# Two graph-attention and feed-forward layers on one core: the rates of the feed-forward's first normalisation move to ScalarE and GpSimd, and its draining slots leave the written order

## The chip, the cores and the metric

The kernel runs on one core of a Trainium2 chip, as one launch. The metric is the device time of that launch in microseconds (us). A core has five engines with their own instruction queues: TensorE (PE in the profile; its weight loads are PEld), VectorE (DVE), ScalarE (ACT), GpSimd (POOL) and SyncE (SP), which here only issues transfers. Each queue is worked off in order, and engines wait for each other through semaphores.

## The reference

The input `x` has 4096 rows of 256 numbers, the adjacency matrix `adj` is 4096 x 4096. There are two layers, each a graph attention and a feed-forward, both with a residual and with a layer normalisation ahead:

```python
x = x + L0_gnn(layernorm(x), adj)      # 4 heads of 64, masked softmax
x = x + L0_ffn(layernorm(x))           # the stage that is changed
x = x + L1_gnn(layernorm(x), adj)      # two attentions, one after the other
x = x + L1_ffn(layernorm(x))           # router, 2 of 6 experts per row
```

The feed-forward of layer 0 is a recurrence of 30 steps on each row, with one weight matrix `W` (256 x 256):

```python
def step(h):
    h = h + 0.01 * tanh(h)
    h = h * sigmoid(h)                                   # Silu
    h = (h - mean) * rsqrt(var + 1e-5) * ln_w + ln_b     # over the 256 columns
    return h @ W.T + b
```

Rows don't influence one another in this stage. Its input is `layernorm(x1)`, where `x1` is the output of the first attention.

## The kernel before

**Tiling.** A tile is 128 rows (one per partition) by 256 columns. Four tiles make a group (`G = 4`, 512 rows), eight groups make the whole input (`NG = 8`). In the feed-forward a *unit* is one step of one group: `units = 30 * 8 = 240`, unit `u` works on group `u % 8`. The state of all rows stays in the buffer `y`, scaled by 100.

**Slots.** The loop over `at` (246 slots) is a software pipeline. In slot `at` unit `at` begins (Tanh on ScalarE at L861, the addition `th` on GpSimd at L862); unit `at - 2` goes through Silu (L850), a scaled float16 copy of its right half (L852), the remainder of that copy on VectorE (L853, called `lower`), a transposing transfer on SP's queue (L857), and its statistics (L874 and L876, VectorE); unit `at - 3` has its left half transposed on TensorE (L831) and copied out of PSUM (L881, ScalarE), and its rate (variance plus eps) to the power of -0.5 formed (L884 ScalarE, L885 and L886 GpSimd); unit `at - 4` is multiplied by the weights (L896 in float32, L899 in float16); unit `at - 5` is written to `y` (L838, VectorE). Slots 0 to 7 are the first pass over the groups, in which the later stages fill; slots 240 to 245 drain.

**First normalisation.** Before its first Tanh a group must be normalised into `y`. `load(g)` takes the rows of `x1` from DRAM (SP's queue, four buffers in the pool `stream`, shared with other stages); `measure(g)` calls `over_std`: statistics (L101, L103), the addition of eps (L105) on VectorE, the power (L106) on GpSimd; `init(g)` makes `rs` (times 100, L726) and `nm` (minus mean times `rs`, L728) on VectorE, then four activations write `y` (L730, ScalarE). Groups 0 and 1 are measured ahead of the loop; in slot `at`, `init(at + 1)` stands ahead of `measure(at + 2)`.

**Weight preparation.** Ahead of the loop VectorE and TensorE fold `ln_w` and `ln_b` into the weights and find a power of two to scale them (L749 to L805). The first scaled copy (L852 of unit 0) needs that `scale`. Parts of the preparation, the end of the first attention and the first slots share VectorE's queue.

**Order.** Around the slot loop stands `tc.manual_schedule` for PE, DVE, ACT and POOL: these engines' queues get the instructions in the order in which the loop writes them. Outside it a planner decides, from its own costs and due times, the order in each queue. SP isn't in the list. `add_manual_dep` makes the addition at L862 wait for `lower` of the unit two before, with the reason "the port that both use".

**The drain.** For the units of the last step, `y` is written with the residual's scale, `load(u % NG)` brings `x1` back, GpSimd adds it (L912) and SP stores the sum to `x2d` (L913), from which the next attention loads its rows (L93).

Of the kernel before, what the change touches and what calls it, by code (L numbers as in the profile page):

```python
# [11 lines left out]
F32 = mybir.dt.float32  # L12
BF16 = mybir.dt.bfloat16
F16 = mybir.dt.float16
I32 = mybir.dt.int32
AF = mybir.ActivationFunctionType
OP = mybir.AluOpType
# [4 lines left out]
P = 128  # L22
C = 256
# [4 lines left out]
G = 4  # L28
EPS = 1e-5
# [15 lines left out]
def gnn_ffn_kernel(ctx: ExitStack, tc: tile.TileContext, a: dict, out: bass.AP):  # L45
    nc = tc.nc
# [3 lines left out]
    NG = NT // G  # L50
    GR = G * P
# [30 lines left out]
    def rows_of(t, g):  # L82
        return t[g * GR : (g + 1) * GR, :].rearrange("(r p) c -> p r c", p=P)
# [12 lines left out]
    def over_std(pool, src):  # L96

        st = pool.tile([P, G, 6], F32, name="ln_st")
        mv = pool.tile([P, G, 2], F32, name="ln_mv")
        for r in range(G):  # L100
            nc.vector.bn_stats(st[:, r, :], src[:, r, :])  # L101
        for r in range(G):
            nc.vector.bn_aggr(mv[:, r, :], st[:, r, :])  # L103
        rstd = pool.tile([P, G], F32, name="ln_rstd")
        nc.vector.tensor_scalar(rstd, mv[:, :, 1], EPS, None, op0=OP.add)  # L105
        nc.gpsimd.tensor_tensor(rstd, rstd, mhalf, OP.pow)  # L106
        return rstd, mv
# [588 lines left out]
    with ExitStack() as scope:  # L696
# [2 lines left out]
        w16 = one.tile([P, 2, C], F16, name="w16")  # L699
        scale = one.tile([P, 2], F32, name="scale")  # L700
        under = one.tile([P, 2, G], F32, name="under")
        eps = one.tile([P, 1], F32, name="eps")
        nc.gpsimd.memset(eps, EPS)
        bias = one.tile([P, C], F32, name="bias")
        last = one.tile([P, C], F32, name="last")
        y = one.tile([P, NT, C], F32, name="y")
# [5 lines left out]
        def load(g):  # L712
            if g not in ahead:
                load_ahead(x1d, g)
            x1[g] = ahead.pop(g)

        measured = {}

        def measure(g):
            measured[g] = over_std(small, x1[g])  # L720

        def init(g):
            t = x1.pop(g)
            rstd, mv = measured.pop(g)
            rs = small.tile([P, G], F32, name="rs")
            nc.vector.tensor_scalar(rs, rstd, 100.0, None, op0=OP.mult)  # L726
            nm = small.tile([P, G], F32, name="nm")
            nc.vector.scalar_tensor_tensor(nm, mv[:, :, 0], -1.0, rs, op0=OP.mult, op1=OP.mult)  # L728
            for r in range(G):
                nc.scalar.activation(  # L730
                    y[:, g * G + r, :], t[:, r, :], AF.Identity, scale=rs[:, r : r + 1], bias=nm[:, r : r + 1]
                )

        for g in range(3):
            load(g)
        with tc.tile_pool(name="f_prep", bufs=1) as prep, tc.tile_pool(name="f_pps", bufs=1, space=PSUM) as pps:
            ln = prep.tile([2 * KC, P], F32, name="ln")
# [2 lines left out]
            wr = prep.tile([P, KC, C], F32, name="wr")  # L740
            nc.scalar.dma_start(wr, a["L0_ffn_W"].rearrange("(k p) c -> p k c", p=P))
            nc.scalar.dma_start(bias, bcast_rows(a["L0_ffn_b"]))
            measure(0)
            init(0)
            measure(1)
            ps = pps.tile([P, 2 * KC], F32, name="ps_ln")
            nc.tensor.transpose(ps, ln, ident[: 2 * KC, : 2 * KC])
            lnT = prep.tile([P, 2 * KC], F32, name="lnT")
# [63 lines left out]

        th, zs, mvs, rs, zT, zT16, pos = {}, {}, {}, {}, {}, {}, {}
        units = FFN_STEPS * NG
        with tc.manual_schedule(
            engines={
                mybir.EngineType.PE,
                mybir.EngineType.DVE,
                mybir.EngineType.Activation,
                mybir.EngineType.Pool,  # L820
            }
        ):
            for at in range(units + 6):
                if at + 3 < NG:
                    load(at + 3)
                u = at - 3
                if 0 <= u < units:
                    z = zs.pop(u)
                    pt = ps_t.tile([P, GR], F32, name="tp")
                    for r in range(G):  # L830
                        nc.tensor.transpose(pt[:, r * P : (r + 1) * P], z[:, r, :P], ident)  # L831
                u = at - 5
                if 0 <= u < units:
                    g = u % NG
                    po, rstd = pos.pop(u), rs.pop(u)
                    end = u >= units - NG
                    for r in range(G):
                        nc.vector.scalar_tensor_tensor(  # L838
                            y[:, g * G + r, :],
                            po[:, r, :],  # L840
                            rstd[:, r : r + 1],
                            last if end else bias,
                            op0=OP.mult,
                            op1=OP.add,
                        )
                u = at - 2
                lower = None
                if 0 <= u < units:
                    z = zs[u] = work.tile([P, G, C], F32, name="z")
                    nc.scalar.activation(z, th.pop(u), AF.Silu, scale=0.01)  # L850
                    z16 = work.tile([P, 2, G, P], F16, name="z16", bufs=4)
                    nc.scalar.activation(z16[:, 0], z[:, :, P:], AF.Identity, scale=scale[:, :1])  # L852
                    lower = nc.vector.scalar_tensor_tensor(  # L853
                        z16[:, 1], z[:, :, P:], scale[:, :1], z16[:, 0], op0=OP.mult, op1=OP.subtract
                    )
                    zT16[u] = work.tile([P, 2 * G, P], F16, name="zT16", bufs=4)
                    nc.sync.dma_start_transpose(zT16[u], z16.rearrange("p s r c -> p (s r c)"))  # L857
                if at < units:
                    g = at % NG
                    th[at] = work.tile([P, G, C], F32, name="th", bufs=4)  # L860
                    nc.scalar.activation(th[at], y[:, g * G : (g + 1) * G, :], AF.Tanh, scale=0.01)  # L861
                    ins = nc.gpsimd.tensor_tensor(th[at], th[at], y[:, g * G : (g + 1) * G, :], OP.add)  # L862
                    if lower is not None:
                        tc.add_manual_dep(
                            ins.ins,
                            lower.ins.name,
                            mybir.DependencyInfo(mybir.DependencyClass.Sync, mybir.DependencyReason.DATA),
                            reason="the port that both use",
                        )
                if 0 <= u < units:  # L870
                    st = small.tile([P, G, 6], F32, name="z_st")
                    mv = small.tile([P, G, 2], F32, name="z_mv")
                    for r in range(G):
                        nc.vector.bn_stats(st[:, r, :], z[:, r, :])  # L874
                    for r in range(G):
                        nc.vector.bn_aggr(mv[:, r, :], st[:, r, :])  # L876
                    mvs[u] = mv
                u = at - 3
                if 0 <= u < units:
                    zT[u] = work.tile([P, GR], F32, name="zT")  # L880
                    nc.scalar.copy(zT[u], pt)  # L881

                    rs[u] = small.tile([P, G], F32, name="z_rs")
                    nc.scalar.activation(rs[u], mvs.pop(u)[:, :, 1], AF.Identity, bias=eps)  # L884
                    nc.gpsimd.tensor_tensor(rs[u], rs[u], mhalf, OP.pow)  # L885
                    nc.gpsimd.tensor_tensor(rs[u], rs[u], under[:, int(u >= units - NG), :], OP.mult)  # L886
                if at + 1 < NG:
                    init(at + 1)
                if at + 2 < NG:
                    measure(at + 2)  # L890
                u = at - 4
                if 0 <= u < units:
                    src, src16 = zT.pop(u), zT16.pop(u)
                    po = pos[u] = ps_o.tile([P, G, C], F32, name="po")
                    for r in range(G):
                        nc.tensor.matmul(po[:, r, :], src[:, r * P : (r + 1) * P], wT, start=True, stop=False)  # L896
                        for part in range(2):
                            for other in range(2):
                                nc.tensor.matmul(  # L899
                                    po[:, r, :],  # L900
                                    src16[:, part * G + r, :],
                                    w16[:, other, :],
                                    start=False,
                                    stop=(part == 1 and other == 1),
                                )
                    if u >= units - NG:
                        load(u % NG)
                u = at - 5
                if units - NG <= u < units:
                    g = u % NG  # L910
                    t = x1.pop(g)
                    nc.gpsimd.tensor_tensor(t, t, y[:, g * G : (g + 1) * G, :], OP.add)  # L912
                    nc.sync.dma_start(rows_of(x2d, g), t)  # L913


    RH = a["L1_ffn_router_w1"].shape[1]
# [456 lines left out]
```

## Time and profile before

| | us |
|---|---|
| median of 3 runs | 3432.09 (3427.78 to 3432.75) |
| profiled execution, own time | 3432.09 |
| its span, on which all profile times lie | 3430.3 |
| feed-forward: first init to last addition of rows | 800.0 to 1797.5 |
| filling: first init to the steady pace | 800 to about 865 |
| steady pace, per unit | 3.92 |
| draining: last Tanh to the first transpose of the next attention | 1765.03 to 1795.90 |

In the profile's rows a line reads: start (us from the span's start), duration, engine, line of the kernel, operation, output<-inputs, shapes, count; in brackets the idle time of the engine just before and what ended it. In the chain of waits the columns are start, length and what was running. Durations of neighbours on one engine overlap by some 0.1 us, so a sum over a queue is made from starts.

### The profile page before, as it was taken

The numbers are of one execution on the slowest core, as the hardware profiler recorded it, in microseconds if no ns is written. First come the engines' busy times: TensorE is split into PE (matmuls) and PEld (weight loads), VectorE is DVE, ScalarE is ACT, GpSimd is POOL, SyncE is SP. The second block draws the span as 40 slices with busy tenths as digits, with TensorE's granted clock in tenths as the row PEclk, the third lists the DMA queues.
The fourth block names the chain that finished last, engine by engine and source line by source line (L and its number), as shares of the span: only waits on it lengthen the run. The fifth ranks groups of instructions, "written<-read, shape, count | busy, mean of one in ns | idle before, by whom it ended". The sixth has DMA issues, their size and how long they took to land.

```text
span 3430.3 us, 84143 instructions
## 1 busy us (share of the span) xinstructions
PE 3156.7 (92%) x34367; PEld 2771.3 (81%) x34367; DVE 3115.3 (91%) x6016; ACT 2754.3 (80%) x3414; POOL 1242.3 (36%) x1149
## 2 busy tenths in 40 slices
PE   7889999996999999999988999999989999985995
PEld 4788888884888888888876999999779999983884
DVE  7999999998999999999988999999889999996445
ACT  3888888896888888888866999999799999982221
POOL 3211100003999999999992000000200000002662
PEclk9999999997999999999999999999999999996997
DMA  7997886603333333333354031230503041314224
GB/s 146 173 228 152 184 184 142 192 22 77 68 67 68 69 69 69 69 69 68 67 140 147 22 123 58 90 118 24 167 24 124 27 136 43 120 46 145 88 91 185
DMA packets 533658, 351.62 MB, mean 103 GB/s; under 512 B 350589, under 2 KB 483866, under 8 KB 533274
## 3 DMA queue, kind: packets, MB, share of 16 engines
q1 hardware_dynamic: 452210, 287.12, 30.4%
q0 software_dynamic: 73920, 52.97, 9.9%
q10 hardware_dynamic: 7144, 6.16, 0.6%
q8 instruction: 271, 4.44, 0.5%
q14 instruction: 113, 0.93, 0.1%
HBM read 248.01 MB, written 68.81 MB: 92 GB/s over the span
## 4 chain that ended last, share of the span: by engine, by line
PE 36%; DVE 35%; issue 13%; POOL 7%; ACT 6%; DMA 2%; DVEq 0%; POOLq 0%; ACTq 0%; SPq 0%
DVE m L617 17%; PE acc L569 10%; PE po L899 9%; PE po L896 9%; ACT st L483 4%; DVE rows L632 3%; PE tp L831 2%; DVE m L632 2%; POOL th L862 2%; PE ph L1262 1%; POOL yd L1293 1%; DVE z_st L874 1%; DVE y L838 1%; POOL gx L1227 1%; DVE u L496 1%
## 5 line engine op out<-in xcount | busy, mean ns | idle before, releaser
L569 PE MATMUL acc<-vals,m 128*128 128x130 f16 (+1 forms) x19456 | 1722.4, 233 | 72.0 <-DVE m L632 42.5
L483 ACT ACTIVATE st<-f1b,f2b 128x1024 bf16<-128x1024 f32 (+2 forms) x1664 | 1659.1, 1073 | 98.8 <-DVE m L617 92.1
L569 PEld LDWEIGHTS <-m 128*128 128x128 bf16 x19456 | 1517.3, 98 | 170.2 <-DVE m L632 64.8
L617 DVE TENSOR_TENSOR m<-st,m 128x2048 bf16<-128x2048 bf16 (+2 forms) x832 | 929.1, 1134 | 15.2 <-ACT st L483 14.9
L569 PE MATMUL acc<-vals,rows 128*128 128x130 f16 x5120 | 614.1, 221 | 15.1 <-DVE rows L632 15.1
L899 PE MATMUL po<-w,zT 128*128 128x256 f16 x3840 | 580.4, 274 | 5.7 <-DMA zT<-z 5.7
L896 PE MATMUL po<-wT,zT 128*128 128x256 f32 x1920 | 579.1, 384 | 6.4 <-ACT zT L881 6.4
L862 POOL TENSOR_TENSOR th<-th,y 128x1024 f32<-128x1024 f32 x240 | 568.8, 2370 | 38.4 <-ACT th L861 14.8
L899 PEld LDWEIGHTS <-zT 128*128 128x128 f16 x3840 | 377.6, 98 | 169.7 <-DMA zT<-z 7.3
L569 PEld LDWEIGHTS <-rows 128*128 128x128 bf16 x5120 | 490.0, 96 | 20.5 <-DVE rows L632 20.1
L632 DVE TENSOR_TENSOR rows<-m,m 128x2048 bf16<-128x2048 bf16 x320 | 391.7, 1224 | 10.2
L838 DVE SCALAR_TENSOR_TENSOR y<-po,z_rs,bias 128x256 f32<-128x256 f32 x928 | 384.8, 477 | 4.2 <-PE po L899 2.1
L874 DVE BATCH_NORM_STATS2 z_st<-z 128x6 f32<-128x256 f32 x960 | 335.5, 412 | 0.0
L896 PEld LDWEIGHTS po<-wT,zT 128*128 128x128 f32 x1920 | 292.5, 193 | 16.4 <-ACT zT L881 7.8
L106 POOL TENSOR_TENSOR ln_rstd<-ln_rstd,mhalf 128x4 f32<-128x4 f32 x32 | 42.1, 1317 | 656.8 <-DVE ln_rstd L105 641.9
L850 ACT ACTIVATE z<-th 128x1024 f32<-128x1024 f32 x240 | 251.2, 1046 | 7.3 <-POOL th L862 6.6
L209 POOL DMA_DIRECT2D rows<-in_adj_dram x80 | 72.9, 912 | 492.9 <-PE tp_m L219 479.4
L861 ACT ACTIVATE th<-y 128x1024 f32<-128x1024 f32 x240 | 249.8, 1041 | 0.1
L885 POOL TENSOR_TENSOR z_rs<-z_rs,mhalf 128x4 f32<-128x4 f32 x240 | 244.5, 1019 | 0.0
L881 ACT COPY zT<-tp 128x512 f32<-128x512 f32 x240 | 140.8, 587 | 116.2 <-PE tp L831 116.2
L632 DVE TENSOR_TENSOR m<-m,m 128x1792 bf16<-128x1792 bf16 (+1 forms) x200 | 202.2, 1011 | 13.0 <-PE acc L569 0.5
L462 POOL MEMSET hs<- 128x4 f32 x3 | 0.3, 103 | 582.4 <-DVE u L513 582.3
(246 smaller groups left out, 3159.1 us busy)
## 6 DMA issues: line engine op xcount, KB each, us to landing
m<-edges SPq DMA_DIRECT2D x32, 2048.0 KB
rows<-in_adj_dram POOLq DMA_DIRECT2D x64, 448.0 KB
edges<-ms SPq DMA_DIRECT2D x64, 448.0 KB
m<-edges SPq DMA_DIRECT2D x16, 1792.0 KB
f1b<-fd SPq DMA_DIRECT2D x32, 512.0 KB
rows<-x1d SPq DMA_DIRECT2D x16, 512.0 KB
y<-yd SPq DMA_DIRECT2D x16, 512.0 KB
f1b<-fd SPq DMA_DIRECT2D x16, 448.0 KB
```

Of the source, the lines that this page charges most:

```text
L483: nc.scalar.activation(steps[at][:, s, :w], f1b[c, h][:, :w], AF.Relu, bias=f2b[:, 2 * q + s, h : h + 1], scale=BIG)
L569: nc.tensor.matmul(acc[:, i, cols], lhs[:, s, rows], v[:, cols], start=(j == 0 and n_ == 0), stop=(j == NT - 1 and n_ == 1), skip_group_ch ...
L617: nc.vector.tensor_tensor(m1[:, :, :w], st[:, :, :w], m, OP.logical_and if turned(q) else OP.min)
L632: nc.vector.tensor_tensor(m2[:, :, :w], m, m1[:, :, :w], OP.subtract)
L838: nc.vector.scalar_tensor_tensor(y[:, g * G + r, :], po[:, r, :], rstd[:, r : r + 1], last if end else bias, op0=OP.mult, op1=OP.add,)
L850: nc.scalar.activation(z, th.pop(u), AF.Silu, scale=0.01)
L861: nc.scalar.activation(th[at], y[:, g * G : (g + 1) * G, :], AF.Tanh, scale=0.01)
L862: ins = nc.gpsimd.tensor_tensor(th[at], th[at], y[:, g * G : (g + 1) * G, :], OP.add)
L874: nc.vector.bn_stats(st[:, r, :], z[:, r, :])
L885: nc.gpsimd.tensor_tensor(rs[u], rs[u], mhalf, OP.pow)
L896: nc.tensor.matmul(po[:, r, :], src[:, r * P : (r + 1) * P], wT, start=True, stop=False)
L899: nc.tensor.matmul(po[:, r, :], src16[:, part * G + r, :], w16[:, other, :], start=False, stop=(part == 1 and other == 1),)
```

## The change

The statistics of a group stay on VectorE (`measure`), but what follows them is a new function `rate`: one activation on ScalarE scales the variance and eps by 1e-4 (so that the power gives 100 times the rate), and three GpSimd operations form the power, mean times rate, and its negative. VectorE's three small operations per group are gone. `measure`, `rate` and `init` of one group now stand in three successive slots, so the statistics are taken one slot earlier and groups 0 to 2 ahead of the loop; `load(3)` goes ahead too. The loop's body becomes a function `slot(at)`, the same but for these calls; slots 0 to 239 are called inside `tc.manual_schedule`, slots 240 to 245 after it, so that the planner orders them.

```diff
-        eps = one.tile([P, 1], F32, name="eps")
-        nc.gpsimd.memset(eps, EPS)
+        eps = one.tile([P, 2], F32, name="eps")
+        nc.gpsimd.memset(eps[:, :1], EPS)
+        nc.gpsimd.memset(eps[:, 1:], EPS * 1e-4)
...
-        measured = {}
+        measured, rates = {}, {}
 
         def measure(g):
-            measured[g] = over_std(small, x1[g])
+            st = small.tile([P, G, 6], F32, name="x_st")
+            mv = measured[g] = small.tile([P, G, 2], F32, name="x_mv")
+            for r in range(G):
+                nc.vector.bn_stats(st[:, r, :], x1[g][:, r, :])
+            for r in range(G):
+                nc.vector.bn_aggr(mv[:, r, :], st[:, r, :])
+
+        def rate(g):
+
+            mv = measured.pop(g)
+            rs = small.tile([P, G], F32, name="x_rs")
+            nc.scalar.activation(rs, mv[:, :, 1], AF.Identity, scale=1e-4, bias=eps[:, 1:])
+            nc.gpsimd.tensor_tensor(rs, rs, mhalf, OP.pow)
+            nm = small.tile([P, G], F32, name="x_nm")
+            nc.gpsimd.tensor_tensor(nm, mv[:, :, 0], rs, OP.mult)
+            nc.gpsimd.tensor_scalar(nm, nm, -1.0, None, op0=OP.mult)
+            rates[g] = rs, nm
 
         def init(g):
             t = x1.pop(g)
-            rstd, mv = measured.pop(g)
-            rs = small.tile([P, G], F32, name="rs")
-            nc.vector.tensor_scalar(rs, rstd, 100.0, None, op0=OP.mult)
-            nm = small.tile([P, G], F32, name="nm")
-            nc.vector.scalar_tensor_tensor(nm, mv[:, :, 0], -1.0, rs, op0=OP.mult, op1=OP.mult)
+            rs, nm = rates.pop(g)
...
-        for g in range(3):
+        for g in range(4):
             load(g)
...
-            measure(0)
+            for g in range(3):
+                measure(g)
+                if g < 2:
+                    rate(g)
             init(0)
-            measure(1)
...
+        def slot(at):
+            if 0 < at and at + 3 < NG:
+                load(at + 3)
...
+                nc.scalar.activation(rs[u], mvs.pop(u)[:, :, 1], AF.Identity, bias=eps[:, :1])
...
+            if at + 2 < NG:
+                rate(at + 2)
+            if at + 1 < NG:
+                init(at + 1)
+            if at + 3 < NG:
+                measure(at + 3)
...
-            for at in range(units + 6):
-                if at + 3 < NG:
-                    load(at + 3)
...
-                if at + 1 < NG:
-                    init(at + 1)
-                if at + 2 < NG:
-                    measure(at + 2)
...
+            for at in range(units):
+                slot(at)
+
+        for at in range(units, units + 6):
+            slot(at)
```

In the queues as built, TensorE's order is the same as before throughout, and GpSimd's is the same from the end of the filling on. In the drain ScalarE's Silu of units 238 and 239 stands ahead of the copies of 236 and 237, VectorE's `lower` of 238 and 239 ahead of the writing of `y` for 235 and 236, and on SP the transposing transfer of unit 239 ahead of the load of rows for group 6. `load(3)` is at the same place in SP's queue as before.

## The prediction

> **What bounds the kernel now.** I read the stage windows first, to see where the feed-forward leaves its own pace. Columns: stretch, length, busy time of each engine with its instructions, granted TensorE clock, DMA share, GB/s.
>
> ```profile
> core 0: us, PE busy (x) PEld busy (x) DVE busy (x) ACT busy (x) POOL busy (x), PEclk, DMA share, GB/s
> 800.00:840.00 40.00, 19.00 (x72) 12.12 (x72) 32.98 (x119) 25.32 (x41) 20.10 (x16) 0.59 0.37 93
> 840.00:880.00 40.00, 33.14 (x196) 25.03 (x197) 34.55 (x114) 33.16 (x51) 28.18 (x24) 0.87 0.38 86
> 1000.00:1200.00 200.00, 200.00 (x1430) 163.80 (x1429) 199.35 (x664) 173.82 (x256) 191.21 (x154) 1.00 0.39 68
> ...
> 1750.00:1800.00 50.00, 40.57 (x262) 31.59 (x261) 37.64 (x120) 21.46 (x34) 45.40 (x34) 0.92 0.67 186
> ```
>
> From 880 to 1750 TensorE never rests: 3.92 us per unit (866 us of the stage), untouched by the change. What can move are the filling slots (800 to 865) and the draining ones (1765 to 1796).
>
> In ScalarE's timeline one filling slot runs from Silu to Silu, 832.31 to 839.73, 7.41 us:
>
> ```profile
> 832.31 1.04 ACT L850 ACTIVATE z<-th 128x1024 f32<-128x1024 f32 x1
> 833.38 0.72 ACT L852 ACTIVATE z<-z,scale 128x512 f16<-128x512 f32 x1
> 834.01 1.04 ACT L861 ACTIVATE th<-y 128x1024 f32<-128x1024 f32 x1
> 834.96 0.56 ACT L881 COPY zT<-tp 128x512 f32<-128x512 f32 x1
> 835.42 0.30 ACT L884 ACTIVATE z_rs<-z_mv,eps 128x4 f32<-128x4 f32 x1
> 837.74 2.08 ACT L730 ACTIVATE y<-rows,nm,rs 128x256 f32<-128x256 f32 x4 [2.02 <-DVE nm L728]
> ```
>
> 2.02 us are a wait for `nm`. VectorE's timeline shows why, with GpSimd's addition below it:
>
> ```profile
> 803.31 2.31 DVE L726 TENSOR_SCALAR rs<-ln_rstd 128x4 f32<-128x4 f32 x1 [0.33 <-POOL ln_rstd L106]
> ...
> 809.21 2.24 DVE L728 SCALAR_TENSOR_TENSOR nm<-ln_mv,rs 128x4 f32<-128x4 f32 x1
> ...
> 836.40 1.11 DVE L726 TENSOR_SCALAR rs<-ln_rstd 128x4 f32<-128x4 f32 x1
> ```
> ```profile
> 803.24 2.35 POOL L862 TENSOR_TENSOR th<-th,y 128x1024 f32<-128x1024 f32 x1
> ...
> 835.13 2.35 POOL L862 TENSOR_TENSOR th<-th,y 128x1024 f32<-128x1024 f32 x1 [1.95 <-ACT th L861]
> 837.44 1.01 POOL L885 TENSOR_TENSOR z_rs<-z_rs,mhalf 128x4 f32<-128x4 f32 x1
> 838.53 0.20 POOL L886 TENSOR_TENSOR z_rs<-z_rs,under 128x4 f32<-128x4 f32 x1
> ```
>
> A 0.17 us operation lasts until GpSimd's 2.35 us addition ends. So each slot closes a ring: init (ACT), Silu, scaled copy, `lower` and statistics (DVE), `rs` held to the end of `th` (POOL), `nm`, next init. The early stalls (2.31, 2.24) also lie in VectorE's queue ahead of the weight preparation, whose `scale` is done at 818.46; the first scaled copy waits 2.63 us for it (starts 818.56).
>
> The chain of waits for the drain:
>
> ```profile
> 1784.88 2.31 POOL rows L912
> 1787.21 4.11 DMA x2d<-rows
> 1791.33 4.43 DMA rows<-x2d
> 1795.90 1.96 PE tp L114 x8
> ```
>
> Before 1784.88 it runs through GpSimd alone, gapless from 1756.90 in its timeline.
>
> **The filling, part by part.** Removed from VectorE per group: L105, L726, L728 (0.17, 0.17, 0.15 unblocked). Added: on ScalarE one 128x4 activation (nearest row L884: 0.30, of which 0.20 until the next starts); on GpSimd a multiplication (nearest L886: 0.20, next about 0.1 later) and a tensor_scalar (no row in the filling; the 128x16 tensor_scalar of the attention, L337, is 0.27 free and 1.31 blocked). The power stays. I take 0.25 and 0.3 with their gaps; both at a power's price (1.02, next 1.1 later) would add 1.65 to a slot's GpSimd sum.
>
> (a) *Preparation.* In VectorE's new order the first statistics end at 801.2 (before 801.9: 0.49 us of waiting and four small operations are gone), but a third group comes in ahead of the weights and a fourth right after `lbb` (4 x 0.33 + 0.28 = 1.6 each), so `lbb` is done at 803.8 against 802.97. `th` of unit 0 moves from 803.24 to about 804.1, behind two groups' rates on GpSimd. The first L765 (TENSOR_SCALAR, 128x256) arrives at 805.2 and, like L726, is held to 806.45; the second runs at 807.5, the mean's matmuls end at 809.1 (1.23 after it, as before), L772 at 810.8 (held by `th` of unit 1), its matmuls 2.08 later, then the same chain: `scale` at 816.2, gain 2.3. If L763 or L770 falls under the second `th`, 1.5 us of it are lost; I set off 0.8. The loads of groups 4 to 6 wait for init to free a buffer; before, the first is issued at 802.17 and its data have moved by 806, so its statistics at 806.9 don't wait. Group 3's load is only written earlier: on SP it already stood ahead.
>
> (b) *Slots.* init of group g takes its rates from the slot before, so the 2.70 us idle ahead of init at 822.92 and the 2.02 of the later slots go. The slot becomes ScalarE's own sum of starts: 1.07 + 0.63 + 0.95 + 0.47 + 0.20 + 0.20 (new) + 2.0 = 5.52. Slot 3 (Silu at 824.91 before) starts at 816.2 + 0.7 + 0.95 + 0.2 + 2.0 = 820.1. Four slots, 4 x 5.52, reach slot 7 at 842.2 (before 854.55): 12.4 us. Is another engine slower? GpSimd: 2.35 + 1.1 + 0.25 + 1.1 + 0.25 + 0.3 = 5.35. VectorE: 1.6 (y) + 0.67 + 1.6 + 1.6 = 5.5 at most. Rates are done 2.7 + 2.35 + 3.0 = 8.05 after their slot's start and wanted at 5.52 + 3.5 = 9.0: 1 us of slack, which hides the three GpSimd operations; without it each us is a us per slot.
>
> (c) *TensorE's clock.* Before, the last filling unit ran slow:
>
> ```profile
> 855.64 0.65 PE L831 MATMUL tp<-ident,z 128*128 128x128 f32 x4 [1.50 <-ACT z L850]
> 857.81 1.22 PE L896 MATMUL po<-wT,zT 128*128 128x256 f32 x2 [1.52 <-ACT zT L881]
> 858.83 1.06 PE L899 MATMUL po<-w,zT 128*128 128x256 f16 x4
> ```
>
> Pairs of groups take 1.7 instead of 0.87, so unit 4 (857.81) cost 6.95 and unit 5 began at 864.76. After: unit 4 begins when zT is copied, 842.2 + 1.07 + 0.63 + 0.95 + 0.57 = 845.4; at full clock unit 5 follows at 849.4, 15.4 us earlier than 864.76, and the steady pace carries that to the end. At the slow clock from unit 3 on, unit 5 comes near 854.3: gain 10.4. The row: slow periods began after 3.7 us with only 0.65 us of work in them (two gaps of 1.5); after one gap of 1.52 at 848.88 it stayed fast. The Trainium skill ("TensorE: Matmul & The Clock Gate", HAM oscillation) asks only that no idle gap exceed some 3.4 us; by that these slow periods should not be there, and neither would any after. By the row, what counts is the share of work in such a stretch: 3.9 of 5.5 us from now on, so fast too, but with less certainty. By the page 15.4, by the row's pessimistic reading 10.4; I take fast.
>
> A second rule speaks against moving work to GpSimd: "SBUF — State Buffer" (two separate sides) says that the port pair of VectorE and GpSimd is an exclusive lock for a whole instruction. The rows agree: in steady state L886 takes 0.41 instead of 0.20 beside `lower` (0.74). By the free rows the three operations cost the slot nothing; by the rule up to 0.7 us once a slot, inside the 1 us of slack, so again nothing.
>
> **The drain.** TensorE's and GpSimd's orders there are unchanged. ScalarE puts Silu of 238 ahead of 236's zT copy: copy from 1766.56 to 1770.4, and L896 from 1770.28 to 1771.0, hidden since L899 waits for zT's transfer to 1771.43. 237's copy comes after Silu of 239 (1771.04 to 1777.3): L899 starts 1778.3 instead of 1777.80, hidden by the next transfer at 1784.64; uncovered it is 0.5. VectorE puts `lower` ahead of `y` twice, but GpSimd's additions hold `lower` to about the old times, and the `y` behind it (up to 3 us late) is wanted by GpSimd only at 1784.83. On SP the last transposing transfer passes a 512 KB load (0.46): perhaps 1 us for unit 239, yet what follows it (rows added at 1795.15, stored 1797.53) is the last group of the next stage; the load then is 2 us late for an addition at 1790.7. The chain through 1787.21 doesn't feel any of it. I take 0, between -1.5 and +1.
>
> **Sum.** 15.4 - 0.8 + 0 = 14.6 us. Profiled: span 3430.3, own time 3432.09 (1.8 around it), equal to the median of three. 3432.1 - 14.6 = **3417.5 us**.
>
> **Rivals.** *A, slow clock from unit 3* (0.17): gain 10.4 - 0.8 = 9.6, 3422.5. For: it fell back twice in this stretch; against: 74% work. *B, GpSimd becomes the bound* (0.08): nm, neg at a power's price and locked by `lower`, slot 5.35 + 1.65 + 0.7 = 7.7, as long as before; what stays is (a), the init wait of slot 2 and unit 4: 2.3 + 2.5 + 3.0 - 4 x 0.3 - 0.8 = 5.8, 3426.3. *C, slower* (0.03): the same queue, each of the new operations held as L726 was, by 2.3 us. Gain turns to loss at 4 x (X - 7.41) > 7.0, a slot of X = 9.2, and is a measurable loss from 10.9; three holds of 2.3 give 5.35 + 6.9 = 12.3 and 3432 - 7 + 19.6 = 3444.7. Against: VectorE has no locking operation over 0.75 us in a slot. *D, the drain gives too* (0.07): the transfer's 1.5 us reach the chain, 3416. The forecast itself: 0.65, own range 3413 to 3420.
>
> **Numbers.** 0.2% (6.9 us) is about what a measurement here tells from no change. Forecast, A and D are faster: 0.89; B same: 0.08; C slower: 0.03. The range of eight in ten reaches up to A with 1.5 us more (3424), and down by the 4.3 us that the fastest run before lay under its median, plus D (3411.5).
>
> **What would show it.** ScalarE's init rows without idle time after `nm` and slots of 5.5 us; `scale` near 816; TensorE's unit 5 near 849; the drain from the last Tanh to the first `tp` L114 still 30.9 us (1765.03 to 1795.90). Wrong if idle time before init names `x_nm`, if TensorE's groups stay at 1.06 us after 840, or if `rows` in the chain moved against the last Tanh.

## The result, and the profile after

| | kernel before | changed kernel |
|---|---|---|
| median, us | 3432.85 (3427.78 to 3434.89, 6 runs) | 3418.38 (3416.52 to 3422.26, 6 runs) |
| ratio | 1 | 0.9961, 95% interval 0.9948 to 0.9973 |
| profiled execution: own time, span | 3432.09, 3430.3 | 3416.70, 3415.0 |
| the same pair measured again later, median | 3436.49 (18 runs) | 3425.16 (6 runs), ratio 0.9969 (0.9957 to 0.9982) |

By the medians the change gains 14.5 us (3417.5 was forecast) and, measured again, 11.3 us.

The stage windows of the changed kernel, in the columns of those shown before; the last one is moved with the drain.

```profile
800.00:840.00 40.00, 23.67 (x106) 16.27 (x107) 31.86 (x126) 34.81 (x62) 30.79 (x36) 0.64 0.48 125
840.00:880.00 40.00, 38.90 (x278) 31.59 (x277) 38.60 (x135) 38.02 (x57) 36.92 (x31) 1.00 0.46 81
1000.00:1200.00 200.00, 200.00 (x1430) 163.77 (x1429) 199.36 (x665) 173.62 (x256) 191.61 (x154) 1.00 0.40 68
1735.00:1785.00 50.00, 37.96 (x254) 29.72 (x254) 38.39 (x115) 20.71 (x33) 44.21 (x34) 0.96 0.64 179
```

The steady stretch (1000 to 1200) is what it was. From 840 on TensorE runs at full clock (0.87 before) and is busy for 38.9 of 40 us (33.1 before): the filling is over some 15 us sooner.

One filling slot in ScalarE's timeline of the changed kernel, Silu to Silu:

```profile
825.39 1.04 ACT L857 ACTIVATE z<-th 128x1024 f32<-128x1024 f32 x1
826.47 0.72 ACT L859 ACTIVATE z<-z,scale 128x512 f16<-128x512 f32 x1
827.09 1.04 ACT L868 ACTIVATE th<-y 128x1024 f32<-128x1024 f32 x1
828.04 0.57 ACT L888 COPY zT<-tp 128x512 f32<-128x512 f32 x1
828.51 0.30 ACT L891 ACTIVATE z_rs<-z_mv,eps 128x4 f32<-128x4 f32 x1
828.71 0.28 ACT L732 ACTIVATE x_rs<-x_mv,eps 128x4 f32<-128x4 f32 x1
828.89 2.06 ACT L743 ACTIVATE y<-rows,x_nm,x_rs 128x256 f32<-128x256 f32 x4
830.86 1.04 ACT L857 ACTIVATE z<-th 128x1024 f32<-128x1024 f32 x1
```

No idle time is left ahead of L743: the slot takes 5.47 us instead of 7.41. GpSimd in the same slot:

```profile
825.06 1.03 POOL L892 TENSOR_TENSOR z_rs<-z_rs,mhalf 128x4 f32<-128x4 f32 x1
826.17 0.20 POOL L893 TENSOR_TENSOR z_rs<-z_rs,under 128x4 f32<-128x4 f32 x1
826.32 1.01 POOL L733 TENSOR_TENSOR x_rs<-x_rs,mhalf 128x4 f32<-128x4 f32 x1
827.41 0.62 POOL L735 TENSOR_TENSOR x_nm<-x_mv,x_rs 128x4 f32<-128x4 f32 x1
828.12 0.23 POOL L736 TENSOR_SCALAR x_nm<-x_nm 128x4 f32<-128x4 f32 x1
828.31 2.36 POOL L869 TENSOR_TENSOR th<-th,y 128x1024 f32<-128x1024 f32 x1
830.63 1.04 POOL L892 TENSOR_TENSOR z_rs<-z_rs,mhalf 128x4 f32<-128x4 f32 x1
```

It has no gap either. The product `x_nm` takes 0.62 us where VectorE's `lower` (827.22 to 827.97) runs beside it, and 0.20 us where only VectorE's statistics do (at 803.96).

TensorE's unit 4, slow before, and the start of unit 5 (lines left out between):

```profile
844.89 0.70 PE L905 MATMUL po<-wT,zT 128*128 128x256 f32 x2 [1.10 <-ACT zT L888]
845.42 0.60 PE L908 MATMUL po<-w,zT 128*128 128x256 f16 x4
...
848.91 0.60 PE L905 MATMUL po<-wT,zT 128*128 128x256 f32 x2
```

The unit takes 4.02 us instead of 6.95. And the drain, in the chain of waits:

```profile
1769.05 2.31 POOL rows L921
1771.37 4.41 DMA x2d<-rows
1775.80 5.30 DMA rows<-x2d
...
1781.23 1.96 PE tp L114 x8
```

The last Tanh starts at 1749.18, so the stretch from it to this `tp` is 32.05 us, 1.2 more than before. GpSimd's part is as long as it was (22.19 us to the end of `rows`, 22.18 before); the store and the load take 9.71 us together instead of 8.54.

**Three lengths to compare runs by.** Medians of these runs don't tell 4 us apart. Three lengths inside the profile do: from ScalarE's first load of `ln` (L738 before, L751 after; ahead of what is changed in this stage) to the first scaled copy; from there to the last Tanh; from there to the first `tp` of the next attention. The first two are equal to 0.05 us between profiles of kernels that have the same filling. All runs, in us (a slot is Silu to Silu in the filling):

| kernel | ratio to before (95%) | slot | `ln` load to scaled copy | to last Tanh | to `tp` L114 |
|---|---|---|---|---|---|
| before | 1 | 7.41 | 24.56 | 946.47 | 30.87 |
| changed | 0.9961 (0.9948 to 0.9973) | 5.47 | 22.85 | 932.98 | 32.05 |
| changed, again | 0.9969 (0.9957 to 0.9982) | 5.47 | 22.85 | 932.98 | 31.33 |
| filling alone | 0.9960 (0.9947 to 0.9974) | 5.47 | 22.83 | 932.97 | 31.94 |
| drain alone | 1.0002 (0.9994 to 1.0011) | 7.41 | 24.53 | 946.51 | 31.81 |
| three slots, rates on VectorE | 0.9979 (0.9972 to 0.9985) | 5.28 | 27.80 | 933.11 | 31.96 |
| rates off VectorE, in init's slot | 1.0041 (1.0026 to 1.0056) | 10.01 | 26.09 | 958.05 | 30.95 |
| filling, two more powers | 0.9982 (0.9974 to 0.9989) | 7.20 | 22.84 | 938.94 | 32.01 |
| before, 20 products in slots 4 to 7 | 0.9999 (0.9991 to 1.0007) | 7.41 | 24.53 | 945.20 | 31.28 |
| before, 20 products in slots 4 to 9 | 0.9995 (0.9986 to 1.0003) | 7.41 | 24.54 | 945.27 | 30.83 |
| filling, additions on VectorE | 0.9965 (0.9952 to 0.9979) | 5.47 | 22.85 | 932.98 | 29.56 |
| the same, late rates on VectorE | 0.9965 (0.9951 to 0.9979) | 5.28 | 22.81 | 933.39 | 30.12 |

The change took 1.71 us from the first length and 13.49 from the second, 15.2 in all. Of the 13.49, 10.56 lie between the first scaled copy and the start of TensorE's unit 4 (39.25 us before, 28.69 after) and 2.93 in unit 4 itself (6.95 and 4.02).

### The profile page after: what moved, and what is told of

It reads as the page before. It is cut to its first block, busy times and chain, and to the rows that moved or that the text cites. A ratio compares the mean times of both kernels' runs of the same rounds, so it can differ in the third digit from the quotient of the medians.

```text
span 3415.0 us, 84150 instructions
## 1 busy us (share of the span) xinstructions
PE 3149.6 (92%) x34367; PEld 2767.7 (81%) x34367; DVE 3105.9 (91%) x5992; ACT 2754.6 (81%) x3422; POOL 1248.2 (37%) x1166
## 4 chain that ended last, share of the span: by engine, by line
DVE 32%; POOL 31%; issue 15%; PE 14%; ACT 6%; DMA 2%; ACTq 0%; DVEq 0%; POOLq 0%; SPq 0%
DVE m L617 17%; POOL th L869 16%; PE acc L569 10%; POOL z_rs L892 7%; ACT st L483 4%; POOL z_rs L893 3%; DVE rows L632 3%; DVE m L632 2%; POOL yd L1316 2%; POOL gx L1250 2%; DVE u L496 1%; DVE v L382 1%; DVE ms L229 1%; PE ph L308 1%; DVE u L506 1%
## 5 line engine op out<-in xcount | busy, mean ns | idle before, releaser
L617 DVE TENSOR_TENSOR m<-st,m 128x2048 bf16<-128x2048 bf16 (+2 forms) x832 | 929.1, 1134 | 15.2 <-ACT st L483 14.9
L106 POOL TENSOR_TENSOR ln_rstd<-ln_rstd,mhalf 128x4 f32<-128x4 f32 x24 | 34.1, 1421 | 645.4 <-DVE ln_rstd L105 630.5
L632 DVE TENSOR_TENSOR m<-m,m 128x1792 bf16<-128x1792 bf16 (+1 forms) x200 | 202.2, 1011 | 13.1 <-PE acc L569 0.5
```

The lines of the kernel that those rows point to most:

```text
L617: nc.vector.tensor_tensor(m1[:, :, :w], st[:, :, :w], m, OP.logical_and if turned(q) else OP.min)
L632: nc.vector.tensor_tensor(m2[:, :, :w], m, m1[:, :, :w], OP.subtract)
```

## The experiments

**The two halves of the change.** *Filling alone* (`fill_only` where an expectation names it) is the changed kernel with the draining slots back in the written order; *drain alone* is the kernel before with only those slots out of it.

```diff
# filling alone, against the changed kernel
-            for at in range(units):
+            for at in range(units + 6):
                 slot(at)
-
-        for at in range(units, units + 6):
-            slot(at)
# drain alone, against the kernel before; the loop's body becomes slot(at)
-            for at in range(units + 6):
...
+            for at in range(units):
+                slot(at)
+
+        for at in range(units, units + 6):
+            slot(at)
```

> The change's filling alone; the draining slots stand in the written order again. Theory (the filling gave all, and the drain cost 1.2 us because SP's queue issues the load of rows for group 6 in front of the stores and loads that the next attention waits for): unit 5 on TensorE near 849 as in the changed kernel, the stretch from the last Tanh to the next attention's first transpose back from 32.05 to 30.9 us, time 3417.2 us, 1.2 us below the changed kernel. Rival (the drain outside the written order gave part of the gain): the stretch at 32 or more, and the time above 3420.

> The kernel before, with only slots 240 to 245 taken out of the written order. Theory: unit 5 on TensorE still near 865, the stretch from the last Tanh to the next attention's first transpose 32.05 instead of 30.87 us, time 3434 us against 3432.9 before, within what can be told. Rival (the drain gains): stretch under 30 us, time 3430 or below.

The filling alone has the whole gain: 0.9960, lengths of 22.83 and 932.97 us. The drain alone has none: 1.0002, within 0.1% either way. But the stretch at the end is 31.94 us with the *written* order, so the 1.2 us of the changed kernel's profile do not belong to the new order. The chain of waits of *filling alone*:

```profile
1770.88 4.25 DMA x2d<-rows
...
1775.15 5.36 DMA rows<-x2d
```

and of the changed kernel run again:

```profile
1769.99 4.39 DMA x2d<-rows
...
1774.40 4.61 DMA rows<-x2d
```

> The changed kernel as it is, beside the two others. Theory (the order of the draining slots costs and gains nothing; what differs at the end is the time of one store and one load, 8.5 to 9.8 us together): from the scale's first use on ScalarE to the next stage's first transposition 963.8 to 965.1 us, the last Tanh to that transposition anywhere between 30.9 and 32.1 us. Rival (the order costs 1.2 us by bringing a load of group 6 past the store): 32.0 us again, and the store and the load of the last pair at 9.6 us or more. Ratio to the kernel before 0.996 by both.

The same 512 KB load takes 5.36 us in the old order and 4.61 in the new one. Over the profiles with the additions on GpSimd the stretch is 30.83 to 32.01 us in the written order (seven) and 31.33 to 32.05 in the new one (three). A difference of a few tenths can't be excluded; 1.2 us of cost by the load of group 6, which SP issues behind the last transposing transfer (20.9 us after the last Tanh instead of 19.1), is not borne out.

**The two halves of the filling.** *Three slots, rates on VectorE* keeps measure, rate and init in three successive slots but makes the rates with VectorE's operations of before. *Rates off VectorE, in init's slot* makes them on ScalarE and GpSimd, directly ahead of init. Both have the drain in the written order.

```diff
# three slots, rates on VectorE: against the changed kernel
         def measure(g):
-            st = small.tile([P, G, 6], F32, name="x_st")
...
+            measured[g] = over_std(small, x1[g])
         def rate(g):
-            nc.scalar.activation(rs, mv[:, :, 1], AF.Identity, scale=1e-4, bias=eps[:, 1:])
-            nc.gpsimd.tensor_tensor(rs, rs, mhalf, OP.pow)
...
+            nc.vector.tensor_scalar(rs, rstd, 100.0, None, op0=OP.mult)
+            nc.vector.scalar_tensor_tensor(nm, mv[:, :, 0], -1.0, rs, op0=OP.mult, op1=OP.mult)
# rates off VectorE, in init's slot: against the changed kernel
-            for g in range(3):
-                measure(g)
-                if g < 2:
-                    rate(g)
+            measure(0)
+            rate(0)
             init(0)
+            measure(1)
...
-            if at + 2 < NG:
-                rate(at + 2)
             if at + 1 < NG:
+                rate(at + 1)
                 init(at + 1)
-            if at + 3 < NG:
-                measure(at + 3)
+            if at + 2 < NG:
+                measure(at + 2)
```

> Measure, rate and init in three successive slots, but the rates formed as before: eps, rs and nm on VectorE, the power on GpSimd; drain in the written order. Theory (the ring through init is what cost the slot, and it is opened by the slot of distance, not by freeing VectorE): slots of 5.3 us on ScalarE without idle time before init, scale back near 818 because rs and nm are held by GpSimd's additions again in the preparation, gain 12 to 13 us, 3420 to 3421. Rival (VectorE's small operations are the cost wherever they stand): slots stay at 7.4 us and the time near 3430.

> Rates on ScalarE and GpSimd as in the change, but in the slot of init, right ahead of it, with the statistics one slot before as in the old kernel; drain in the written order. Theory (the slot of distance is what opens the ring): the ring is now Silu, copy, Tanh 2.7, th 2.35, the unit's rate 1.35, the group's rate 1.65, init 2.0: slots of 10 us, idle time before init put down to x_nm, unit 5 on TensorE near 875, time 3440 to 3446. Rival (freeing VectorE of the small operations is enough): slots of 5.5 us and a time near 3418.

From the `ln` load to the last Tanh the four combinations stand so, in us against the kernel before:

| | init in the rate's slot | measure, rate, init in three slots |
|---|---|---|
| rates on VectorE | 0 (before) | -10.1 |
| rates on ScalarE and GpSimd | +13.1 | -15.2 (changed) |

Taking VectorE out of the rates is a loss by itself: the slot then waits for `th`, two powers and three small operations in a row on GpSimd. ScalarE's timeline of *rates off VectorE, in init's slot*:

```profile
842.71 2.07 ACT L743 ACTIVATE y<-rows,x_nm,x_rs 128x256 f32<-128x256 f32 x4 [4.43 <-POOL x_nm L736]
```

Idle time of 4.43 us names `x_nm`, the slot is 10.01 us, unit 5 on TensorE starts at 874.78 (near 875 was expected), and the kernel is slower than before by 0.26 to 0.56%, 12.2 us by the medians (3448.49 against 3436.28). The three slots are what removes the wait. With them even the rates on VectorE leave ScalarE without a wait: slots of 5.28 us, 0.19 less than the changed kernel, which is the ScalarE activation that VectorE's way doesn't need. What the rates on VectorE cost lies ahead of the slots. VectorE's timeline of *three slots, rates on VectorE*, and GpSimd's:

```profile
803.04 2.30 DVE L726 TENSOR_SCALAR x_rs<-ln_rstd 128x4 f32<-128x4 f32 x1 [0.80 <-POOL ln_rstd L106]
...
811.23 2.31 DVE L726 TENSOR_SCALAR x_rs<-ln_rstd 128x4 f32<-128x4 f32 x1
```
```profile
802.98 2.34 POOL L861 TENSOR_TENSOR th<-th,y 128x1024 f32<-128x1024 f32 x1
...
811.16 2.36 POOL L861 TENSOR_TENSOR th<-th,y 128x1024 f32<-128x1024 f32 x1
```

Twice a 0.17 us operation lasts as long as the addition beside it: 4.3 us lost in the queue in which the weight preparation follows. `scale` is first used 27.80 us after the `ln` load instead of 22.85. The kernel before has two such holds too, and 24.56 us; but there the first one stands behind `lbb`, here ahead of it (`lbb` is done 14.3 us after the `ln` load instead of 9.0). The run's gain of 6.5 us by the medians (3428.76 against 3435.22; 5.2 to 9.6 by the ratio's interval, 9.0 by the three lengths) is less than the 12 to 13 expected. The expectation had `scale` as early as in the kernel before, and these 3.24 us are the largest part of what is missing.

**How much room GpSimd has.** *Filling, two more powers* adds, to the rates of groups 4 to 7, two powers whose result is not used.

```diff
# against filling alone
             nc.gpsimd.tensor_tensor(rs, rs, mhalf, OP.pow)
+            if g >= 4:
+                more = small.tile([P, G], F32, name="more")
+                for _ in range(2):
+                    nc.gpsimd.tensor_tensor(more, rs, mhalf, OP.pow)
```

> As fill_only, with two more powers (128x4, some 1.1 us each, result unused) on GpSimd in the rate of groups 4 to 7. In the changed kernel's trace GpSimd is gapless in slots 3 to 6, 5.47 us like ScalarE. Theory (its queue has no room left, only the ring had): each of these slots grows by the full 2.2 us, unit 5 near 856.5, time about 3425; 3428 if TensorE's clock falls back in the longer slots. The prediction's reading (1 us of slack a slot hides as much): 4 x 1.2 = 4.8 us, 3422.

The two powers take 2.09 us in GpSimd's queue and lengthen the slot from 5.47 to 7.20, by 1.73, between the 1.2 and the 2.2 of the two readings; ScalarE now waits for `x_nm`, and the product, no longer beside `lower`, is back at 0.20 us. GpSimd in one such slot, then ScalarE's init:

```profile
837.99 2.35 POOL L873 TENSOR_TENSOR th<-th,y 128x1024 f32<-128x1024 f32 x1
...
842.65 2.09 POOL L737 TENSOR_TENSOR more<-x_rs,mhalf 128x4 f32<-128x4 f32 x2
844.71 0.20 POOL L739 TENSOR_TENSOR x_nm<-x_mv,x_rs 128x4 f32<-128x4 f32 x1
```
```profile
845.26 2.08 ACT L747 ACTIVATE y<-rows,x_nm,x_rs 128x256 f32<-128x256 f32 x4 [1.81 <-POOL x_nm L740]
```

Taken by starts, GpSimd's own work in a slot of the changed kernel is therefore 7.20 - 2.06 (842.65 to 844.71) = 5.14 us against ScalarE's 5.47: some 0.3 us of room. In the changed kernel the time for which `lower` holds `x_nm` (0.3 to 0.4 us) fills it, which is why GpSimd has no gap and the slot is still ScalarE's sum. From the first scaled copy to the last Tanh the run is 5.97 us longer than *filling alone*: one slot of 6.03 and three of 7.20 to 7.22 stand where that has three of 5.47 and a last one of 5.29. TensorE's clock did fall back, in unit 3 (843.30 to 849.4), but unit 4 has its `zT` only at 850.45 and then runs at full clock, so this cost nothing.

**TensorE's clock by itself.** The kernel before, with matrix products of 128x128 whose result is not used, ten behind the transpositions and ten at the slot's end, first in slots 4 to 7, then in slots 4 to 9.

```diff
# against the kernel before
+        ps_d = scope.enter_context(tc.tile_pool(name="f_psd", bufs=1, space=PSUM))
+        def busy(at):
+            if 4 <= at <= 7:        # second run: 4 <= at <= 9
+                pd = ps_d.tile([P, P], F32, name="pd")
+                for _ in range(10):
+                    nc.tensor.matmul(pd, ident16, ident16, start=True, stop=True)
```

> The kernel before, with 20 small matmuls (128x128, bf16, into a PSUM tile that nobody reads) in each of slots 4 to 7, placed in TensorE's idle time. Theory (3.0 us of the gain are unit 4 at full clock, because the share of work in a stretch sets the clock): groups of unit 4 at 0.87 instead of 1.7 us a pair, unit 5 at 861.8 instead of 864.8, time 3.0 us below before, 3429.9. Rival (the clock there is hidden, or doesn't follow the small matmuls): 3432.9.

> The kernel before with 20 matrix products of 128x128 whose result is not used in each of the slots 4 to 9. Theory (TensorE's late clock in unit 4 sets the start of unit 5): no slow pair in unit 4, which takes 4.0 us instead of 6.95, and the last Tanh comes 943.6 us after the scale's first use instead of 946.5, so 2.9 us less; the median 2.9 us less, which is less than this comparison can resolve. Rival (the slots alone set it): unit 4 is quicker but the last Tanh stays at 946.5. Where the products with idle space before slot 8 are too few to hold the clock, slow pairs remain and the gain is their number times 0.42 us less.

TensorE's timeline around unit 4 in the first of the two:

```profile
852.65 0.72 PE L817 MATMUL pd<-ident 128*128 128x128 bf16 x10
854.29 0.66 PE L838 MATMUL tp<-ident,z 128*128 128x128 f32 x4 [0.93 <-ACT z L858]
856.47 0.70 PE L904 MATMUL po<-wT,zT 128*128 128x256 f32 x2 [1.51 <-ACT zT L889]
857.57 1.06 PE L904 MATMUL po<-wT,zT 128*128 128x256 f32 x2
...
860.85 0.60 PE L904 MATMUL po<-wT,zT 128*128 128x256 f32 x2
```

The products stopped one slot too early: between the idle products and 856.47 TensorE has idle times of 0.93 and 1.51 us with 0.66 us of work between them, and it is slow from about 857.1 to 860.6. Unit 4 takes 5.69 us instead of 6.95 (the time from its start to that of unit 5), 1.26 less, and the last Tanh comes 1.27 us sooner. With the products carried on, in the second run:

```profile
860.59 0.60 PE L904 MATMUL po<-wT,zT 128*128 128x256 f32 x2
...
863.21 0.72 PE L817 MATMUL pd<-ident 128*128 128x128 bf16 x10
863.76 0.61 PE L838 MATMUL tp<-ident,z 128*128 128x128 f32 x4
864.21 0.72 PE L817 MATMUL pd<-ident 128*128 128x128 bf16 x10
864.77 0.65 PE L904 MATMUL po<-wT,zT 128*128 128x256 f32 x2
```

No slow pair is left in unit 4 (859.62 to 863.21), but the last Tanh comes only 1.20 us sooner, not 2.9 as expected. The difference is the price of the probe, which the expectation had left out: TensorE is now the bound, and three batches of ten products, 0.55 us each by their starts (863.21 to 863.76, 864.21 to 864.77, and one at 868.30), stand in its way. 2.93 - 3 x 0.55 = 1.28. So in both runs the end follows TensorE's time in this unit to 0.1 us; that the full 2.93 us arrive when nothing is paid for them is what the sum of the changed kernel shows (10.56 + 2.93 = 13.49). The medians (0.9999 and 0.9995) can't resolve 1.2 us.

**A better drain.** Since GpSimd's chain sets the drain, *filling, additions on VectorE* moves the last step's residual additions (L921) there. The second variant also makes the rates of groups 4 to 7 on VectorE, those of groups 0 to 3 staying as in the change.

```diff
# against filling alone
-                nc.gpsimd.tensor_tensor(t, t, y[:, g * G : (g + 1) * G, :], OP.add)
+                nc.vector.tensor_tensor(t, t, y[:, g * G : (g + 1) * G, :], OP.add)
# and in the second variant
         def rate(g):
+            if g >= 4:
+                ...
+                nc.vector.tensor_scalar(rs, rstd, 100.0, None, op0=OP.mult)
+                nc.vector.scalar_tensor_tensor(nm, mv[:, :, 0], -1.0, rs, op0=OP.mult, op1=OP.mult)
```

> As fill_only, and the eight additions of the residual (128x1024) on VectorE instead of GpSimd. Theory (the drain is GpSimd's queue: three additions of th and rates and five of rows before the store that the next stage waits for): VectorE takes some 1.1 us for each instead of 2.35, slots of the drain about 5.0 us, the fifth addition of rows 3.8 us earlier against the last steady slot, time 3413.4. Rival (the drain hangs on the transposing transfers and TensorE): no gain against fill_only, 3417.

> The filling in three slots, with ScalarE and GpSimd making the rates of groups 0 to 3 and VectorE those of groups 4 to 7, and the residual additions of the last step on VectorE. Theory (VectorE's small operations cost only where an addition of th on GpSimd holds them during the preparation): the scale's first use comes 18.6 us after VectorE's softmax product of the stage before, as in the changed kernel (23.4 where VectorE makes all rates), and the filling slots take 5.28 us instead of 5.47; the additions on VectorE leave 29.5 us from the last Tanh to the next stage's transposition instead of 31.9. Together 2.4 to 3.2 us below the changed kernel, a ratio of 0.9952 to the kernel before. Rival (the rates load VectorE in the slots too): slots of 5.5 us or more, with ScalarE idle before its normalisation, and no gain but that of the additions.

The chain of waits of the first variant now passes through VectorE:

```profile
1768.04 1.19 DVE rows L921
...
1769.25 4.75 DMA x2d<-rows
...
1774.02 3.93 DMA rows<-x2d
```

The stretch is 29.56 us (30.12 in the second variant) against 31.94. Of these 2.4 us the additions give 1.4: the store starts 20.7 us after the last Tanh in both variants, 22.2 in *filling alone* (3.8 us sooner was expected). The rest is the spread of the store and the load (8.68 us together against 9.61). The time of the kernel doesn't show it: 0.9965 twice, between the 0.9960 and the 0.9969 of the kernels that ran beside them. With intervals of 0.13% (4.5 us) a gain of 1.4 us is neither shown nor excluded, and what the 1640 us behind this place do with it stays open.

The second variant settles what *three slots, rates on VectorE* had lost: with the rates of the preparation on GpSimd the first scaled copy is back at 22.81 us, and the slots are 5.28 us. Yet the last Tanh is 0.4 us later, not 0.8 earlier. VectorE's queue has no gap from 829 on, with a rate held for 1.73 us in it, so `y` of unit 0 (L855) comes late. Its timeline, and TensorE's:

```profile
829.51 1.73 DVE L735 TENSOR_SCALAR x_rs<-ln_rstd 128x4 f32<-128x4 f32 x1
...
833.14 1.65 DVE L855 SCALAR_TENSOR_TENSOR y<-po,z_rs,bias 128x256 f32<-128x256 f32 x4
```
```profile
834.94 0.67 PE L915 MATMUL po<-wT,zT 128*128 128x256 f32 x2 [2.98 <-ACT y L753]
...
835.88 1.02 PE L915 MATMUL po<-wT,zT 128*128 128x256 f32 x2
...
839.73 0.60 PE L918 MATMUL po<-w,zT 128*128 128x256 f16 x4
```

TensorE's unit 2 has its `zT` at 832.64 but starts at 834.94, just after this `y` ends (834.79). By the kernel it waits for it: the pool `f_pso` has two PSUM buffers, and unit 2 writes into the one that `y` of unit 0 reads. (The profile names ScalarE's normalisation, which ends at the same time and which unit 2 doesn't need.) After this idle time of 2.98 us TensorE is slow from 835.88 to 839.26, and from 834.94 on it has no gap: unit 5 starts 33.12 us after the first scaled copy instead of 32.71, which is the 0.4 us by which the last Tanh is later. What ScalarE's shorter slot gains is lost on TensorE, 2.3 us by the wait and 1.6 by the slow pairs (3.38 us for four groups instead of 1.74), less the idle time that TensorE has in the changed kernel's slots.

## Why the prediction was right

- **Preparation** (gain 2.3, of which 0.8 was set off): measured 1.71. It came by another way than the one described. `lbb` was done at 802.93, not 803.8, so the first TENSOR_SCALAR of the weights (L780) ran at 804.32, just ahead of `th` at 804.44, and was not held. The statistics of group 4, which "don't wait" in the prediction, waited 1.55 us for their rows (806.34); `sq` was held by the second `th` (1.52 us instead of 0.67). What the prediction called the cause, two small operations held for 2.3 us each in the queue of the weights, is shown by *three slots, rates on VectorE*, which has them and loses 4.95 us. So the 0.8 us set off were spent, on `sq` (0.85) instead of the two lines named.
- **Slots** (5.52 us, ScalarE's sum): 5.47, without idle time. The slack behind it was mis-sized. By its method (rates done against rates wanted) it was 1.0 us; measured, `x_nm` is done at 828.35 and init starts at 828.89, 0.54 us. And for added work in GpSimd's queue the room is 0.3 us: the free sum is 5.14 us where 5.35 was estimated, and the hold by `lower` takes up the rest. The exclusive port of the Trainium skill ("SBUF — State Buffer", two separate sides) is seen on `x_nm`, 0.62 against 0.20 us; it cost nothing here only because it had 0.3 us to fall into. Rival B was nearer than 0.08 says: two powers more make GpSimd the bound.
- **TensorE's clock** (unit 4 at full speed, unit 5 at 849.4): unit 4 at 844.89, at full clock, unit 5 at 848.91. Of that 0.65 us is an earlier arrival at the stage (the first `ln` load is at 793.35 instead of 794.00), so 849.56 on the clock of before. The size of this step, 6.95 - 4.02 = 2.93 us, reached the end, as the two runs with idle products confirm for 1.2 us of it from the other side. Rival A, the slow clock from unit 3 on, did not occur: with 3.9 us of work in 5.5 TensorE stayed fast in the four profiles with slots of 5.47 us. But the prediction's reason, the share of work in a stretch, is not shown to be what decides: see the last section. Where TensorE had to wait once for 2.98 us, in a kernel with shorter slots, it fell back, so the step was less safe than its right outcome suggests.
- **Drain** (0, between -1.5 and +1): the profile has +1.2, outside the bound, and not the 30.9 us that was to show it. The sign of being wrong, `rows` moved against the last Tanh, did not occur (22.19 us against 22.18). The order is free as far as can be told, as predicted (1.0002 with the drain alone). What the bound left out is the spread of one store and one load at the end of the chain, 8.5 to 9.7 us from one profile to another in the written order, 9.0 to 9.7 in the new one. Rival D, 1.5 us of gain, did not come: the earlier transfer doesn't reach GpSimd's chain.
- **Sum**: 1.71 + 13.49 = 15.2 us up to the last Tanh, where 15.4 - 0.8 = 14.6 were forecast; medians 14.5 and 11.3. That the first median lies within 0.1 us of the forecast is luck: its interval reaches from 9.3 to 17.9 us. (The lower end of the prediction's range, worked out as it says, is 3417.5 - 1.5 - 4.3 = 3411.7, not 3411.5.)
- **Rival C** (each new operation held for 2.3 us): no hold of one of them in the slots is over 0.42 us, the time of 0.62 us beside `lower` instead of 0.20. Ahead of them, beside `sq`, a power takes 1.49 us instead of 1.03.

## What to carry to other kernels

A software pipeline's slot closes through the chain that must fit into one slot, so spreading a chain over one more slot can be worth more than making its links faster; moving the links to other engines without that was a loss here (+13.1 us), and with it a gain. When two engines share a port, the cost of a small operation can be the length of the other engine's instruction beside it, so look at which queue stands behind it: with the rates on VectorE, holds of up to 1.7 us in the slots left ScalarE without a wait, while two of 2.3 us cost 5 us ahead of the weights. And when the medians can't resolve a term, measure it between two places in the profile whose distance repeats from run to run.

## What the runs showed of the hardware

- TensorE fell to about half speed (pairs of groups 1.7 us instead of 0.87) after two idle times of 0.93 and 1.51 us with 0.66 us of work between them, and stayed slow for about 3.5 us (857.1 to 860.6, before with 20 products in slots 4 to 7). In the kernel before, this came after 1.50 and 1.52 us around 0.65 us of work, for at least 6 us (857.81 to 863.9), and after 1.50 and 1.51 us for some 4 (842.99 to 846.9); in the last variant after a single idle time of 2.98 us, for 3.4 us (835.88 to 839.26), while one of 2.06 us (ahead of 840.44 in *three slots, rates on VectorE*) left it at full speed. The Trainium skill ("TensorE: Matmul & The Clock Gate", HAM oscillation) names idle gaps of over some 3.4 us as what to avoid; none of these is that long. But the share of work in such a stretch does not decide it alone. In *rates off VectorE, in init's slot* the same pattern was followed by full speed:

```profile
855.79 0.66 PE L837 MATMUL tp<-ident,z 128*128 128x128 f32 x4 [1.53 <-ACT z L856]
857.96 0.70 PE L903 MATMUL po<-wT,zT 128*128 128x256 f32 x2 [1.51 <-ACT zT L887]
...
858.93 0.60 PE L903 MATMUL po<-wT,zT 128*128 128x256 f32 x2
```

It was so at 835.77 too, with 1.75 and 1.51 us. Both times TensorE had come back to full speed less than 3 us before (853.22, 832.98). What decides, and what makes the slow period 3.5 or over 6 us long, wasn't tried.
- The same 512 KB load at the end of the chain took from 4.30 to 5.42 us between profiles with the written order of the drain; what decides it wasn't found.
